# A graph network over 100,000 edges: of two steps' running maxima one row is stored, chosen by a masked copy

## The chip, the core and the metric

The kernel runs on one core of a Trainium2 chip. The core has TensorE (PE, matrix products into PSUM), VectorE (DVE, elementwise), ScalarE (ACT), GpSimd (POOL, which here issues the gathers) and SyncE (SP, which issues DMAs). Each engine works through its own list of instructions in order, and waits on semaphores for the others. The metric is the device time of one execution in microseconds (us). Before the change its median over 9 runs is 3999.06 us (3992.29 to 4028.08).

## The reference, cut to what matters

There are N = 6250 nodes with D = 256 features, E = 100,000 edges (src, dst, 64 edge features), and the edges come sorted by dst. Three times, the rows of the source nodes are gathered and their maximum is taken over all edges with the same dst:

```python
# 1: L0_gnn
e = relu((x[dst] - x[src]) @ theta_w.T + theta_b + x[src] @ phi_w.T + phi_b)
x = layernorm(x + where(isfinite(out := segment_max(e, dst, N)), out, 0))
# 2 and 3: L1_gnn, two rounds
hv = x @ W_in + b_in
for W, b in ((W_u0, b_u0), (W_u1, b_u1)):
    msg = segment_max(relu(concat([hv[src], edge_attr_64]) @ W + b), dst, N)
    hv = where(has_in, msg + hv, hv)
x = layernorm(x + relu(hv @ W_ro + b_ro))
```

The nodes have unequal numbers of edges; in the inputs given here one node has no edge and three have exactly one.

## The kernel before, in words

**Tables.** The product with a node's features is made once a node and not once an edge: each of the three sweeps r = 0, 1, 2 has a table in DRAM, `table[r]`, with one row of 256 numbers a node, and an edge fetches the row of its source. Table 0 is made in the prologue (L460 to 593), tables 1 and 2 by the nodes of the sweep before (L926 and the like). In the sweeps 1 and 2 the edge's own 64 features are multiplied and added for each edge.

**Edges.** They are taken in reverse order, padded to 782 x 128 and cut into 14 blocks (13 of 56 steps, one of 54). Within a block each of the 128 lanes (partitions) holds consecutive edges, one a step. So a node's edges lie behind one another in a lane, and may go on in the next lane, or in the next block.

**A step** (the loop at the end of `sweep`, L1010 to 1066). POOL gathers 128 rows of the table, one a lane, into a slot of a `run` tile of eight steps (`sources`, L784 to 792; four such tiles; issued AHEAD = 16 steps early). In sweeps 1 and 2 PE multiplies the features of two steps into a PSUM bank (`pair`, L816 to 831, three banks, issued two pairs early), and DVE adds the gathered rows to the bank (L1030, 512 elements a lane for two steps). Then one DVE instruction a step makes the running maximum along the lane (L1043, 256 elements): `lim` is large where the step's edge has the same dst as the one before and very negative where a new node begins, so the running maximum starts anew there. The result overwrites the gathered row. In sweep 0 a part of the steps takes raw rows of x and multiplies them itself (`raw_turn`, `raw_pair`); the others take table rows as they are.

**The store** (L1047 to 1051). After each eight steps SP stores the whole `run` tile, 1024 KB, to a DRAM array `S`, one row for every edge. The row at a node's last edge is the node's maximum within its lane.

**Block ends.** `over_lanes` (L833 to 860) transposes the lanes' last rows with PE, makes the running maximum over lanes with DVE and transposes it back into `cs` (the last KEPT = 6 blocks are held), so that a node that began in an earlier lane gets that lane's part too.

**Nodes** (L862 to 976). Tiles of 128 nodes, 49 a sweep. `rows` (L870) gathers with POOL the 128 rows of `S` at the nodes' last edges (`end_i`); it waits for all stores of `S` that are pending, and stands in POOL's list among the gathers of the steps. `picks` (L882) and `carried` (L889) fetch the carried part with one-hot matrices and PE, and the node's arithmetic follows in pieces, spread over some ten steps: the maximum (L931), adding (L935), two transposes (L760), a copy by ACT (L762), products (L768), biases (L926, L947), the layernorm (L746 to L755), and the rows of the next table or of the output.

**The order** is written by hand: a table of tasks by step number (`at`), the node schedule at L992 to 997. In sweep 0 DVE and PE also count the edges of each node with one-hot matrices (L707 to 722, the group L710, L716 and L721), 3 steps apart, up to step 320; from the counts `ends_a` and `ends_b` (L727 to 742) work out `end_i`, and only then, from step 324, can sweep 0's nodes begin; they follow at gaps of 6, later 3, steps.

**The check** (L538 to 567): DVE works out from the indices whether the edges are sorted and whether the nodes' tiles lie in the blocks for which the program was laid out. A value is loaded into a register (L588), and if it is not zero, another, general branch of the program (`any_order`) does the work. With the inputs given here the branch `in_order` is taken.

Of the kernel before, what the change touches and what calls it, by code (L numbers as in the profile page):

```python
# [8 lines left out]
F32 = mybir.dt.float32  # L9
BF16 = mybir.dt.bfloat16  # L10
I32 = mybir.dt.int32
# [6 lines left out]
P = 128  # L18
# [31 lines left out]
KEPT = 6  # L50
# [23 lines left out]
def gather_raw(nc, x, x_sb, s_r, i):  # L74

    nc.gpsimd.indirect_dma_start(out=x_sb[:, i, :], out_offset=None, in_=x,
                                 in_offset=bass.IndirectOffsetOnAxis(ap=s_r[:, i:i + 1], axis=0))

# [381 lines left out]
def gnn_kernel(  # L460
    ctx: ExitStack, tc: tile.TileContext, x, xT, src, dst, he, th_wT, th_b, ph_wT, ph_b,
    w_in, b_in, w_u0, b_u0, w_u1, b_u1, w_ro, b_ro, pos, heT, xTn, xn, w_inT, head, near, out,
# [51 lines left out]
    with tc.manual_schedule(), tc.tile_pool(name="pro", bufs=2) as pro, \  # L514
# [23 lines left out]
        def check():  # L538
            down = pro.tile([P, FS], F32, name="down", bufs=1)
            nc.vector.tensor_tensor(down, p_s, d_s, OP.is_lt)  # L540
            downs = pro.tile([P, 1], F32, name="downs", bufs=1)
            nc.vector.tensor_reduce(downs, down, AX.X, OP.max)
# [5 lines left out]
            nc.vector.tensor_max(downs[0:1, :], downs[0:1, :], bad)  # L548
            breaks_p = pps.tile([P, 512], F32, name="breaks_p", bufs=1)
            nc.tensor.matmul(breaks_p[:, :1], every, downs, start=True, stop=True)  # L550
            nc.vector.tensor_copy(breaks, breaks_p[:, :1])
            keep = pro.tile([P, FS], F32, name="down", bufs=1)
            nc.vector.tensor_tensor(keep, p_s, d_s, OP.is_equal)
            alike = BLOCKS.count(BLOCKS[0])
# [33 lines left out]
    bad = nc.values_load(breaks[0:1, 0:1], min_val=0, max_val=P)  # L588
# [8 lines left out]
def in_order(ctx: ExitStack, tc: tile.TileContext, g):  # L597
# [7 lines left out]

    nc = tc.nc
# [4 lines left out]
    part = g["part"]  # L611
# [4 lines left out]
    S = [dram_disjoint_views(nc.dram_tensor(f"S{r}", [FE, D], F32, kind="Internal").ap(), 2) for r in range(3)]  # L616
# [27 lines left out]
    winT = weight(g["w_inT"], "winT")  # L644
    wu0 = weight(g["w_u0"][:D, :], "wu0")
# [40 lines left out]
    def fuse_b():  # L686
        for b, w in ((b2, wu0), (bu1, wu1), (bro, wro)):
            ps = psum.tile([P, 512], F32, tag="pr", name="fuse_p")
            for k in range(2):
                nc.tensor.matmul(ps[:, :D], binT[:, k:k + 1].to_broadcast([P, P]), w[:, k, :], start=(k == 0),  # L690
                                 stop=(k == 1))
            nc.vector.tensor_add(b, b, ps[:, :D])
        nc.vector.tensor_add(tb, tb, pb)

# [48 lines left out]

    def stats(a, name):
# [12 lines left out]
    def turned(a):  # L757
        tp = psum.tile([P, 512], F32, tag="tp", name="tp")
# [12 lines left out]
    def sweep(r):  # L771
# [10 lines left out]
        runs = ahead.pop(r, {})  # L782

        def sources(s, r=r, runs=runs):  # L784
            if s % K == 0:
                runs[s // K] = work.tile([P, K, D], F32, name="run", bufs=4)
            if r == 0 and raw(s) is not None:
# [3 lines left out]
                out=runs[s // K][:, s % K, :], out_offset=None, in_=table[r][:SPARE + 1, :] if early else table[r],  # L791
                in_offset=bass.IndirectOffsetOnAxis(ap=(s_e if early else s_s)[:, s:s + 1], axis=0))

        def raw_turn(i):

            tp = psum.tile([P, 512], F32, tag="tp", name="tp")
# [36 lines left out]
        def over_lanes(b, last):  # L833

            lp = psum.tile([P, 512], F32, tag="tp", name="lp")
# [16 lines left out]
            def back():  # L852
                cp = psum.tile([P, 512], F32, tag="tp", name="cp")
# [8 lines left out]
        def node(t, g, b):  # L862
# [5 lines left out]
            def rows():  # L868
                o["m"] = work.tile([P, D], F32, name="m", bufs=7)
                i = nc.gpsimd.indirect_dma_start(  # L870
                    out=o["m"], out_offset=None, in_=S_r[:P * (FIRST[SPAN[t][1]] + BLOCKS[SPAN[t][1]]), :],
# [107 lines left out]
        if r == 0:  # L979
# [11 lines left out]
            at(begin - 1, ends_b)  # L991
        gap = (6, 4, 6)[r]  # L992
# [15 lines left out]
        for s in range(-AHEAD if r == 0 else 0, FS):  # L1008
# [15 lines left out]
            if s % 2 == 0:  # L1024
                two = runs[c][:, j:j + 2, :].rearrange("p s f -> p (s f)")
                if r > 0:
                    if s + 4 < FS:
                        pair(s // 2 + 2)
                    sums = hp.pop(s // 2)
                    nc.vector.tensor_add(sums, sums, two)  # L1030
                elif raw(s) is not None:
                    sums = hp.pop(s // 2)
# [7 lines left out]
            cur = runs[c][:, j, :]  # L1040
            row = sums[:, s % 2 * D:(s % 2 + 1) * D]
# [5 lines left out]
            if j == K - 1 or s in (FS - 3, FS - 1):  # L1047
                k = 2 if s == FS - 1 else j + 1
                to = S_w[P * FIRST[blk]:P * (FIRST[blk] + BLOCKS[blk]), :].rearrange("(p s) f -> p s f", p=P)
                at_ = s + 1 - k - FIRST[blk]  # L1050
                pending.append(nc.sync.dma_start(to[:, at_:at_ + k, :], runs[c][:, j + 1 - k:j + 1, :]))
# [67 lines left out]
```

## Time and profile before

| what | value |
| --- | --- |
| median of 9 runs | 3999.06 us |
| lowest, highest | 3992.29, 4028.08 us |
| the profiled execution's own time | 4036.09 us |
| its span in the trace | 4034.3 us |
| instructions in the span | 21650 |
| mean granted clock of PE | 0.684 |
| bytes moved | 739.39 MB, 183 GB/s over the span |
| of them, POOL's gathers (queue q0) | 326.92 MB, 27.1% of 16 DMA engines |
| of them, SP's queue, the stores among it (q1) | 337.85 MB, 22.4% |
| of them, ACT's queue, the edge features among it (q10) | 73.16 MB, 5.4% |
| HBM read, written | 404.56 MB, 333.17 MB |

The profile shows one execution, whose own time is 37 us above the median. Its rows give, for a group of like instructions, the line of the kernel, the engine, the operation, what is written and read, the number, the busy time in all and the mean duration in ns, and then the idle time of the engine just before them with what ended most of it. "remote" and "issue" stand for idle time that no instruction or transfer in the trace explains. The table by stage gives for a stretch of the span the busy time and number of instructions of each engine, then the granted clock, the share of the 16 DMA engines that was busy, and the rate. In a timeline the columns are the start, the duration, the engine, the line, the operation, and in brackets the idle time before it with what ended it. PE's ends are modelled and some records can be missing.

The three sweeps lie at about 0 to 1366, 1366 to 2720 and 2720 to 4034 us.

### The profile page before, as it was taken

To read this page: it belongs to the slowest core of one execution; us is meant where nothing else is said; L and a number is where in the kernel's file an instruction comes from. 1 tells how busy PE (TensorE), PEld (TensorE's weight loads), DVE (VectorE), ACT (ScalarE), POOL (GpSimd) and SP (SyncE) were. 2 spreads that over 40 slices of the span, in tenths; PEclk is the share of its full clock that TensorE was granted. 3 is DMA by queue.
4 is the path that set the end of the run, shared out by engine and by line. 5 is a ranking of instruction groups with operands and counts; after the bars stand their busy time and mean duration, and the time that the engine had idled before them with its cause. 6 is when DMAs were issued, how large, how long until landed. Compare 5 with 4: busy or idle time off the path is not lost. (4 is left out here: it accounts for less than half of the span.)

```text
span 4034.3 us, 21650 instructions
## 1 busy us (share of the span) xinstructions
PE 1857.2 (46%) x4631; PEld 821.8 (20%) x4631; DVE 2117.1 (52%) x4750; ACT 237.9 (6%) x618; POOL 2388.2 (59%) x2500
## 2 busy tenths in 40 slices
PE   5452223555520255454545445544545444444455
PEld 4341111222210122221212111122222121211111
DVE  1565554555543365554545456544655665555555
ACT  1000000111100000000000000000000000000000
POOL 5555556666666655655665566655555556666663
PEclk8665555655555577776767677767777878777767
DMA  6456545555555555555655555655555555555554
GB/s 239 161 180 203 187 146 177 176 168 184 169 187 167 177 198 184 188 176 173 201 170 189 166 188 203 211 177 182 180 179 179 184 188 187 189 183 188 189 197 159
DMA packets 241821, 739.39 MB, mean 183 GB/s; under 512 B 52485, under 2 KB 95858, under 8 KB 204434
## 3 DMA queue, kind: packets, MB, share of 16 engines
q0 software_dynamic: 119664, 326.92, 27.1%
q1 hardware_dynamic: 69568, 337.85, 22.4%
q10 hardware_dynamic: 52450, 73.16, 5.4%
q8 instruction: 39, 0.64, 0.1%
q14 instruction: 100, 0.82, 0.1%
HBM read 404.56 MB, written 333.17 MB: 183 GB/s over the span
## 5 line engine op out<-in xcount | busy, mean ns | idle before, releaser
L790 POOL DMA_INDIRECT run<-table,s_s x2258 | 2160.5, 957 | 1276.1 <-issue 656.6
L825 PE MATMUL hp<-whe,hT 128*128 128x512 f32 x1564 | 1007.5, 741 | 769.4 <-DVE run L1043 391.8
L1043 DVE SCALAR_TENSOR_TENSOR run<-run,lim,hp 128x256 f32<-128x256 f32 x1573 | 753.7, 479 | 58.7 <-remote 12.0
L1030 DVE TENSOR_TENSOR hp<-hp,run 128x512 f32<-128x512 f32 x782 | 542.2, 693 | 348.7 <-remote 190.2
L825 PEld LDWEIGHTS hp<-whe,hT 128*128 128x128 f32 x1564 | 298.7, 222 | 1306.9 <-DVE run L1043 725.1
L1043 DVE SCALAR_TENSOR_TENSOR run<-run,lim 128x256 f32<-128x256 f32 x731 | 351.5, 481 | 147.3 <-remote 48.5
L870 POOL DMA_INDIRECT m<-S,end_i x147 | 142.0, 966 | 311.7 <-DMA S<-run 205.3
L889 PE MATMUL v<-cs,pick 128*128 128x256 f32 (+1 forms) x438 | 169.1, 506 | 165.1 <-issue 72.3
L931 DVE TENSOR_TENSOR m<-m,v 128x256 f32<-128x256 f32 x98 | 40.5, 414 | 343.9 <-remote 223.6
L768 PE MATMUL prod<-wcat,aT 128*128 128x512 f32 x196 | 179.7, 1070 | 56.2 <-issue 39.5
L710 DVE TENSOR_TENSOR ol<-col,low 128x1024 bf16<-128x1024 bf16 x98 | 118.8, 1213 | 133.4 <-remote 123.2
L721 PE MATMUL hist<-oh,ol 128*128 128x8 bf16 (+7 forms) x782 | 34.8, 167 | 298.3 <-DVE oh L716 245.2
L889 PEld LDWEIGHTS v<-cs,pick 128*128 128x128 f32 x438 | 102.4, 255 | 274.4 <-issue 244.9
L768 PE MATMUL prod<-wro,aT 128*128 128x256 f32 x196 | 79.0, 543 | 171.6 <-ACT aT L762 88.5
L947 DVE TENSOR_TENSOR m<-prod,bro 128x256 f32<-128x256 f32 x49 | 20.8, 424 | 227.5 <-remote 93.9
L768 PE MATMUL prod<-wu,aT 128*128 128x256 f32 x196 | 72.0, 502 | 126.4 <-issue 79.1
L760 PE MATMUL tp<-ident,h_sb 128*128 128x128 f32 x196 | 48.3, 335 | 142.1 <-DVE h_sb L935 51.2
L926 DVE TENSOR_TENSOR new<-prod,b 128x256 f32<-128x256 f32 x49 | 20.8, 424 | 175.6 <-PE prod L768 71.6
L721 PEld LDWEIGHTS <-ol 128*128 128x128 bf16 x782 | 36.3, 104 | 323.0 <-DVE ol L710 229.6
L840 PE MATMUL lp<-ident,run 128*128 128x128 f32 x84 | 22.7, 363 | 169.5 <-DVE run L1043 98.0
L762 ACT COPY aT<-tp 128x256 f32<-128x256 f32 x147 | 54.7, 372 | 755.2 <-remote 403.1
L932 ACT ACTIVATE m<-m,has 128x256 f32<-128x256 f32 x98 | 49.7, 508 | 824.5 <-issue 386.7
(131 smaller groups left out, 1385.8 us busy)
## 6 DMA issues: line engine op xcount, KB each, us to landing
S<-run SPq DMA_DIRECT2D x291, 1024.0 KB
hT<-in_heT ACTq DMA_DIRECT2D x196, 256.0 KB
run<-table,s_s POOLq DMA_INDIRECT x2258
table<-new ACTq DMA_DIRECT2D x98, 128.0 KB
xg<-in_xTn SPq DMA_DIRECT2D x7, 896.0 KB
xT<-in_xTn SPq DMA_DIRECT2D x49, 128.0 KB
x_sb<-in_xn SPq DMA_DIRECT2D x7, 896.0 KB
out<-new ACTq DMA_DIRECT2D x48, 128.0 KB
```

What stands on the lines that cost most here:

```text
L710: nc.vector.tensor_tensor(ol[:, :k, :], col.unsqueeze(1).to_broadcast([P, k, P]), low[c // half][:, c % half * K:c % half * K + k].unsquee ...
L721: nc.tensor.matmul(hist[:, t0:t0 + w], ol[:, j, :], oh[:, j, :w], start=False, stop=(c == NG - 1 and j == k - 1))
L760: nc.tensor.transpose(tp[:, k * P:(k + 1) * P], a[:, k * P:(k + 1) * P], ident)
L762: nc.scalar.copy(aT.rearrange("p k e -> p (k e)"), tp[:, :2 * P])
L768: nc.tensor.matmul(ps[:, :n], aT[:, k, :], w[:, k, :], start=(k == 0), stop=(k == 1))
L790: nc.gpsimd.indirect_dma_start(out=runs[s // K][:, s % K, :], out_offset=None, in_=table[r][:SPARE + 1, :] if early else table[r], in_offs ...
L825: nc.tensor.matmul(hp[i], hT[c][:, q, :], whe[r - 1].rearrange("p s f -> p (s f)"), start=True, stop=not early)
L870: i = nc.gpsimd.indirect_dma_start(out=o["m"], out_offset=None, in_=S_r[:P * (FIRST[SPAN[t][1]] + BLOCKS[SPAN[t][1]]), :], in_offset=bass. ...
L889: nc.tensor.matmul(o["v"][:, :N1], p, cs[:, blk % KEPT, :N1], start=(blk == SPAN[t][0]), stop=(blk == SPAN[t][1]))
L932: nc.scalar.activation(o["m"], o["m"], AF.Relu, scale=has[:, t:t + 1])
L1030: nc.vector.tensor_add(sums, sums, two)
L1043: nc.vector.scalar_tensor_tensor(cur, prev, lim[:, s:s + 1], row, OP.min, OP.max)
```

## The change

**Of each two steps one row is stored.** A lane's two neighbouring steps 2q and 2q + 1 shall give one row of `S`. If the second edge belongs to the same node as the first, the row of the second step is kept: it contains the first. If a new node begins at the second edge, the row of the first step is kept: it is the end of its node. The second row is then lost for `S`; as long as the new node goes on in the next pair, nothing is lost by that, since its last row comes later. It is lost only if the node has one edge alone, at an odd position: a "lone" row.

For this the steps of a `run` tile are placed so that the even ones fill its first half and the odd ones its second (`slot`). Ahead of each store one DVE instruction, `copy_predicated`, copies the rows of the second half over those of the first half where the mask `goes_on` says so; the mask has one value a lane and pair, is spread over the 256 features by its access pattern, and lies in a PSUM bank of its own. The store takes the first half: 512 KB in place of 1024 KB, and `S` has one row for two edges and 128 rows more at its head.

**Lone rows are made on their own.** The lone nodes are found in sweep 0 from the counts (`ends_b`, `ends_c`), numbered, and their `end_i` points to the 128 rows at the head of `S`. `find` sends the position of each to the lane of its number: 49 one-hot picks by DVE and 49 matmuls with one column by PE. `found` gathers, from a new input `by_pos`, the features and the source of those edges; `found_b` makes the table index and transposes the features. In each sweep `lone_rows` gathers the 128 table rows and `lone_sums` adds the product of the features (sweeps 1 and 2) and stores the 128 rows. In sweep 0 all nodes start 21 steps later for this.

**The check** also counts the lone rows; if there are more than 128, the general branch is taken.

**Room.** KEPT goes from 6 to 7. The transposes' PSUM tag `tp` has one bank in place of two. Two weights, `winT` and `wu0`, needed until step 12 of sweep 0, lie in two of the four buffers of the tag `hT`.

The diff, with the check, the signatures and the unpacking of names left out:

```diff
-KEPT = 6
+KEPT = 7
+LONE = P
...
+def slot(s):
+    return s % 2 * (K // 2) + s % K // 2
...
-    S = [dram_disjoint_views(nc.dram_tensor(f"S{r}", [FE, D], F32, kind="Internal").ap(), 2) for r in range(3)]
+    S = [dram_disjoint_views(nc.dram_tensor(f"S{r}", [LONE + FE // 2, D], F32, kind="Internal").ap(), 2) for r in range(3)]
...
-    winT = weight(g["w_inT"], "winT")
-    wu0 = weight(g["w_u0"][:D, :], "wu0")
+    winT, wu0 = (work.tile([P, K // 2, P], F32, tag="hT", name=n, bufs=4).rearrange("p (k h) f -> p k (h f)", k=2)
+                 for n in ("winT", "wu0"))
+    nc.scalar.dma_start(winT, g["w_inT"].rearrange("(k p) f -> p k f", p=P))
+    nc.scalar.dma_start(wu0, g["w_u0"][:D, :].rearrange("(k p) f -> p k f", p=P))
...
+    goes_on = psum.tile([P, 512], F32, tag="on", name="goes_on", bufs=1)
+    nc.vector.tensor_scalar(goes_on[:, :FS // 2], lim.rearrange("p (q two) -> p q two", two=2)[:, :, 1], 0.0, None,
+                            OP.is_gt)
...
+        odd_i = one.tile([P, NT], I32, name="odd_i")
+        nc.vector.tensor_scalar(odd_i, end_i, 1, None, OP.bitwise_and)
+        nc.vector.tensor_scalar(end_i, end_i, 1, None, OP.arith_shift_right)
+        nc.vector.scalar_tensor_tensor(lone, cnt, 1.0, odd_i, OP.is_equal, OP.mult)
+        nc.vector.tensor_tensor_scan(incl, ones, lone, 0.0, OP.mult, OP.add)
+        ps = psum.tile([P, 512], F32, tag="pr", name="sums")
+        nc.tensor.matmul(ps[:, :1], above, incl[:, NT - 1:NT], start=True, stop=True)
+        sums.append(ps)
+    lone, number = (one.tile([P, NT], F32, name=n) for n in ("lone", "number"))
+    row = one.tile([P, DE + 2], F32, name="lone_row")
+    lone_s = one.tile([P, 1], I32, name="lone_s")
+    lone_T = one.tile([DE, P], F32, name="lone_T")
+    def ends_c():
+        base = one.tile([P, 1], F32, name="base")
+        nc.vector.tensor_copy(base, sums[1][:, :1])
+        nc.vector.scalar_tensor_tensor(number, incl, base, lone, OP.add, OP.mult)
+        nc.vector.tensor_scalar(number, number, -1.0, None, OP.add)
+        half = one.tile([P, NT], F32, name="half")
+        nc.vector.tensor_scalar(half, end_i, float(LONE), None, OP.add)
+        nc.vector.tensor_sub(incl, number, half)
+        nc.vector.tensor_mul(incl, incl, lone)
+        nc.vector.tensor_add(end_i, half, incl)
+    def find(t):
+        if t == 0:
+            sums.append(psum.tile([P, 512], F32, tag="pr", name="sums"))
+        p = work.tile([P, P], F32, name="pick", bufs=4)
+        nc.vector.tensor_scalar(p, col_f, number[:, t:t + 1], None, OP.is_equal)
+        nc.tensor.matmul(sums[2][:, :1], p, end[:, t:t + 1], start=t == 0, stop=t == NT - 1)
+    def found():
+        at_i = one.tile([P, 1], I32, name="at_i")
+        nc.vector.tensor_copy(at_i, sums[2][:, :1])
+        nc.gpsimd.indirect_dma_start(out=row, out_offset=None, in_=by_pos,
+                                     in_offset=bass.IndirectOffsetOnAxis(ap=at_i, axis=0))
+    def found_b():
+        of = row.bitcast(I32)[:, DE:DE + 1]
+        low_i = one.tile([P, 1], I32, name="low_i")
+        nc.vector.tensor_scalar(low_i, of, float(P), float(TROWS), OP.is_lt, OP.mult)
+        nc.vector.scalar_tensor_tensor(lone_s, of, float(-P), low_i, OP.add, OP.add)
+        ps = psum.tile([P, 512], F32, tag="tp", name="tp", bufs=1)
+        nc.tensor.transpose(ps[:DE, :P], row[:, :DE], ident)
+        nc.scalar.copy(lone_T, ps[:DE, :P])
...
-        tp = psum.tile([P, 512], F32, tag="tp", name="tp")
+        tp = psum.tile([P, 512], F32, tag="tp", name="tp", bufs=1)
...
+        def lone_rows():
+            alone["m"] = work.tile([P, D], F32, name="m", bufs=7)
+            nc.gpsimd.indirect_dma_start(out=alone["m"], out_offset=None, in_=table[r],
+                                         in_offset=bass.IndirectOffsetOnAxis(ap=lone_s, axis=0))
+        def lone_sums():
+            if r > 0:
+                ps = psum.tile([P, 512], F32, tag="pr", name="prod")
+                nc.tensor.matmul(ps[:, :D], lone_T, whe[r - 1][:DE, 0, :], start=True, stop=True)
+                nc.vector.tensor_add(alone["m"], alone["m"], ps[:, :D])
+            pending.append(nc.sync.dma_start(S_w[:LONE, :], alone["m"]))
...
-                out=runs[s // K][:, s % K, :], out_offset=None, in_=table[r][:SPARE + 1, :] if early else table[r],
+                out=runs[s // K][:, slot(s), :], out_offset=None, in_=table[r][:SPARE + 1, :] if early else table[r],
...
-                    out=o["m"], out_offset=None, in_=S_r[:P * (FIRST[SPAN[t][1]] + BLOCKS[SPAN[t][1]]), :],
+                    out=o["m"], out_offset=None, in_=S_r[:LONE + P * (FIRST[SPAN[t][1]] + BLOCKS[SPAN[t][1]]) // 2, :],
...
+            at(begin + 1, ends_c)
+            for t in range(NT):
+                at(begin + 2 + t // 7, find, t)
+            at(begin + 10, found)
+            at(begin + 14, found_b)
+            begin += 16
+        at(max(begin, EARLY + 4), lone_rows)
+        at(max(begin, EARLY + 4) + 4, lone_sums)
+        begin += 5 if r == 0 else 0
...
-                two = runs[c][:, j:j + 2, :].rearrange("p s f -> p (s f)")
+                two = runs[c].rearrange("p (two q) f -> p two q f", two=2)[:, :, j // 2, :]
...
-                to = S_w[P * FIRST[blk]:P * (FIRST[blk] + BLOCKS[blk]), :].rearrange("(p s) f -> p s f", p=P)
-                at_ = s + 1 - k - FIRST[blk]
-                pending.append(nc.sync.dma_start(to[:, at_:at_ + k, :], runs[c][:, j + 1 - k:j + 1, :]))
+                a, n = (j + 1 - k) // 2, k // 2
+                at_ = (s + 1 - k) // 2
+                nc.vector.copy_predicated(
+                    runs[c][:, a:a + n, :], goes_on[:, at_:at_ + n].bitcast(I32).unsqueeze(2).to_broadcast([P, n, D]),
+                    runs[c][:, K // 2 + a:K // 2 + a + n, :])
+                of, to = P * FIRST[blk] // 2, P * (FIRST[blk] + BLOCKS[blk]) // 2
+                to = S_w[LONE + of:LONE + to, :].rearrange("(p q) f -> p q f", p=P)
+                at_ -= FIRST[blk] // 2
+                pending.append(nc.sync.dma_start(to[:, at_:at_ + n, :], runs[c][:, a:a + n, :]))
```

## The prediction

> **What bounds the kernel now.** I read the page's totals and costliest groups first, then the waits, then single stretches of the timeline.
>
> ```profile
> PE 1857.2 (46%) x4631; PEld 821.8 (20%) x4631; DVE 2117.1 (52%) x4750; ACT 237.9 (6%) x618; POOL 2388.2 (59%) x2500
> ...
> L790 POOL DMA_INDIRECT run<-table,s_s x2258 | 2160.5, 957 | 1276.1 <-issue 656.6
> L1043 DVE SCALAR_TENSOR_TENSOR run<-run,lim,hp 128x256 f32<-128x256 f32 x1573 | 753.7, 479 | 58.7 <-remote 12.0
> L1030 DVE TENSOR_TENSOR hp<-hp,run 128x512 f32<-128x512 f32 x782 | 542.2, 693 | 348.7 <-remote 190.2
> L931 DVE TENSOR_TENSOR m<-m,v 128x256 f32<-128x256 f32 x98 | 40.5, 414 | 343.9 <-remote 223.6
> L710 DVE TENSOR_TENSOR ol<-col,low 128x1024 bf16<-128x1024 bf16 x98 | 118.8, 1213 | 133.4 <-remote 123.2
> ```
>
> No engine is full. POOL's gathers start 1.25 us apart (0.95 busy, 0.30 before the next), so 2493 of them need 3116 us of the 4034.3. DVE idles 1917 us, nearly all ahead of lines that read a PE product: L1030 348.7, L931 343.9, L947 227.5, L926 175.6, L710 133.4, L943 104.4, L900 84.4. For gathers it waits little (L1030 34.6 us). Averages hide that the sweeps alternate. One block (56 steps) of sweep 2, in the table by stage:
>
> ```profile
> core 0: us, PE busy (x) PEld busy (x) DVE busy (x) ACT busy (x) POOL busy (x), PEclk, DMA share, GB/s
> 3282.00:3333.00 51.00, 34.62 (x79) 13.57 (x79) 47.68 (x110) 5.40 (x15) 29.15 (x31) 0.93 0.66 221
> 3333.00:3377.00 44.00, 8.26 (x20) 4.50 (x21) 7.84 (x19) 1.30 (x4) 27.43 (x29) 0.60 0.45 144
> ```
>
> In the first stretch DVE is busy 47.68 of 51 us: it is the bound. In the second it does 7.84 us of work in 44. The timelines of DVE and POOL there:
>
> ```profile
> 3332.42 1.00 DVE L1043 SCALAR_TENSOR_TENSOR run<-run,lim,hp 128x256 f32<-128x256 f32 x2
> 3341.80 0.42 DVE L947 TENSOR_TENSOR m<-prod,bro 128x256 f32<-128x256 f32 x1 [8.38 <-remote]
> ...
> 3344.18 0.18 DVE L748 BATCH_NORM_AGGREGATE mv<-st 128x2 f32<-128x6 f32 x1
> 3357.90 0.42 DVE L931 TENSOR_TENSOR m<-m,v 128x256 f32<-128x256 f32 x1 [13.54 <-remote]
> ```
> ```profile
> 3315.81 0.94 POOL L870 DMA_INDIRECT m<-S,end_i  x1 [6.38 <-DMA S<-run]
> ...
> 3368.31 0.94 POOL L790 DMA_INDIRECT run<-table,s_s  x1 [0.30 <-issue]
> 3379.58 0.95 POOL L790 DMA_INDIRECT run<-table,s_s  x1 [10.32 <-DVE run L1043]
> ```
>
> DVE waits 8 to 14 us for PE products whose matmuls the profile shows as finished; the real ends are hidden, since PE's ends are modelled. POOL meanwhile issues without pause from 3315.81 until its run buffers are full at 3369, and DVE is free again at 3377.30, 8 us after POOL stops. Over the other blocks the timeline repeats this: PE turns slow some 17 to 21 us after POOL's last pause of 3 us or more, and recovers 6 to 10 us after the next. Why, no row says. For the sum it matters that the end of a slow stretch is timed by POOL, and that the fast stretch is DVE's.
>
> A rule to weigh here. The Trainium skill (TensorE: Matmul & The Clock Gate, Part 1) says that a quiet PE runs at half clock and is warm again after about 3.4 us of work. The 0.60 agrees with a half clock for part of the stretch, but half rate would make 8.26 us of matmuls 16 at most, not 44; by the page alone the slow stretch is no stall and would hide few copies, which is what I assume anyway.
>
> **The change, part by part.** The profiled execution took 4036.1 us (span 4034.3), 37.0 above the median of 3999.06; I sum against 4036.1 and take 37.0 off at the end.
>
> *The masked copy (added).* One DVE instruction of 4 x 256 = 1024 elements ahead of each store of eight steps, 294 to 297 in all. No row shows this operation. The nearest has as many elements: L710, 1213 ns. The f32 rows give the same: (693 - 414)/256 = 1.09 ns an element from L1030 and L931, so 414 + 768 x 1.09 = 1.25 us. Below: 0.69, if it passes two elements at a time (L1030's 512). Above: 2.43, if the selected write costs a second pass. I take 1.21. Behind it on DVE stand the next pair's L1030 and L1043, and SP's store waits for it. Where DVE is idle more than that in the same eight steps, it is hidden. I counted DVE's idle time between neighbouring stores (L1051) in the timeline: it is under 1.25 us in 60 groups of about 98 in sweep 1, 63 of 98 in sweep 2 and 17 of 96 in sweep 0, where PE's counting (L710 waits on it) and POOL leave 2 to 7 us a group. So 123 x 1.21 = **+149** and 17 x 1.21 = **+21**. The slow stretch doesn't absorb the copies ahead of it: DVE enters it some steps behind, POOL ends it at the same time, and those steps are then made up at DVE's pace.
>
> *The store (halved).* 291 stores of 1024 KB become 512 KB: about 154 MB less of 739. DMA is not full (0.66 in the fast stretch) and DVE doesn't wait for gathers, so bytes alone gain nothing. What gains is the landing, for which POOL waits at each block end:
>
> ```profile
> 3309.99 0.32 SPq L1051 DMA_DIRECT2D S<-run  x1
> ...
> 4019.19 0.32 SPq L1051 DMA_DIRECT2D S<-run  x1
> ```
>
> The first (1024 KB) frees POOL's gather at 3315.81, 5.82 us later; the last (256 KB) is followed by its gather at 4021.95, after 2.76. On the line between, 512 KB takes 3.78: 2.04 us less. One block end in each of 14 blocks of sweeps 1 and 2 is on the path, 28 x 2.04 = **-57**. At most all 46 waits of POOL for this store count (30 at L870, 16 at L790): -94; at least 0, if the later copy uses the time up. A rule speaks against halving: the Trainium skill (DMA: Bandwidth & Descriptors, Rules for kernel authors) wants at least 1 MiB a DMA, and its fit of 2.0 us plus bytes at 436 GB/s (Anatomy of one DMA) would save 1.2 us a store, an estimate of -34 in place of -57.
>
> *Lone rows and their search (added).* `find` is 49 picks of 290 ns (L882) and 49 small matmuls of two records each; L889's records are 0.38 us with 256 columns, its weight loads 0.19, so 0.4 to 0.76 us each: 14 us on DVE, 20 to 37 on PE, in seven steps of sweep 0, with four pick buffers between them. I take 15 on the path (0 where POOL's lead is the cover, 60 if a slow PE falls on it). Four gathers more are 4 x 1.25 = 5 us of POOL; the sums, the small stores on SP and the half-dozen index rows are some 3. Together **+23**.
>
> *Edits at no cost.* The check's extra rows (about 4 us by L540's 0.97) lie ahead of POOL's first run gather, which waits 23.4 us for the load of tb until 83.05; uncovered they cost 4. The first node of sweep 0 starts 21 steps later, but by the node schedule the backlog ends at step 636 either way. The slot order changes addresses only. One PSUM bank instead of two for the transposes lets the next wait for ACT's copy (L762, 372 ns); nodes are four steps or more apart, which covers it; uncovered, 147 x 0.37 = 54. Two weights in the hT buffers until step 12: 0 to 5.
>
> **Sum.** 149 + 21 - 57 + 23 = +136: 4036.1 + 136 = 4172, less 37 gives **4135 us**, 3.4% slower.
>
> **Rivals.**
>
> *PE's debt pays for the copies (faster).* If a slow stretch starts after so much PE work, and not after so much time, a slower DVE merely stretches the fast part, and copies fall into PE's 1418 us of waits. For it: the stretches return with the block. Against it: they come in sweep 0 too, with far smaller matmuls. The store's gain then stands alone: 3999 - 94 + 23 = 3928, or 3965 with -57. It decides when fewer than about 28 copies ((57 - 23)/1.21) stay on the path. Chance 0.17, and 0.03 for the next.
>
> *Slow stretches shrink with DMA traffic.* Fewer bytes (21%) would take 0.21 of them: 44 of each 95 us in 2668 us, about 1236, so -260 against +136: about 3875. Against: no store is in flight for most of them, and the DMA share is lower there (0.45).
>
> *A copy of 2.43 us.* 140 x 2.43 = 340 in place of 170: 4305. Only the missing row speaks for it. Chance 0.12.
>
> *About even.* Half of the 140 copies hidden and all 46 landings gained: 85 - 94 + 23 = +14, near 4013. Chance 0.13, of it 0.08 within 0.3% of before.
>
> *The fallback.* More than 128 lone rows would send the kernel into the other branch. The inputs have 3 nodes of one edge, none at an odd position: out.
>
> **How the numbers follow.** The forecast, 4060 to 4270, has 0.55 (copies of 0.69 us on 140 groups, 97 - 57 + 23, make 4062; 1.21 us on six of seven groups of sweeps 1 and 2, and on half of sweep 0's, with no store gain makes 3999 + 203 + 58 + 23 = 4283, cut at 4270). The range 3950 to 4270 leaves out the costly copy (0.12) and the lower part of the faster cases (0.08). About 0.3% is what this measurement can tell from no change: faster 0.20, same 0.08, slower 0.72 (0.55 + 0.12 + 0.05).
>
> **What would show it.** Copies of 1.2 us in DVE's groups; fast stretches of 51 us grown to about 57, slow ones still near 44; POOL's waits for S shorter by 2 us each; POOL's waits for DVE's run longer. I am wrong if the fast stretch keeps its length with the copies in it, if DVE's idle time falls by what the copies add, or if slow stretches get rarer.

## The result and the profile after

The changed kernel takes 4095.31 us (median of 20 runs, 4081.74 to 4108.57), the kernel before 4007.67 us over all 62 runs that stand beside it (3970.11 to 4049.50; the 3999.06 of the table above is the median of nine of them). The ratio is 1.0225, interval 1.0208 to 1.0241: about 90 us slower. The prediction said 4135 us, 3.4% slower.

The profiled execution took 4091.2 us (span 4089.4). From the page of the kernel after, the totals, the queue of the stores and the costliest groups that answer to those shown of before, with the copy as a new one (columns as before: number, busy time, mean ns, idle time before it):

```profile
PE 1901.9 (47%) x4736; PEld 864.2 (21%) x4736; DVE 2495.5 (61%) x5120; ACT 238.4 (6%) x619; POOL 2389.4 (58%) x2504
...
q1 hardware_dynamic: 70000, 184.49, 12.4%
...
L1142 DVE SCALAR_TENSOR_TENSOR run<-run,lim,hp 128x256 f32<-128x256 f32 x1573 | 753.4, 479 | 67.6 <-remote 17.5
L1129 DVE TENSOR_TENSOR hp<-hp,run 128x512 f32<-128x512 f32 x782 | 542.4, 694 | 139.6 <-remote 94.5
...
L1150 DVE COPY_PREDICATED run<-goes_on,run 128x1024 f32<-128x1024 int32 (+1 forms) x297 | 380.8, 1282 | 24.3 <-remote 8.8
...
L1021 DVE TENSOR_TENSOR m<-m,v 128x256 f32<-128x256 f32 x98 | 40.6, 415 | 347.4 <-remote 237.5
...
L739 DVE TENSOR_TENSOR ol<-col,low 128x1024 bf16<-128x1024 bf16 x98 | 118.6, 1210 | 67.0 <-remote 58.8
```

A copy takes 1.28 us; the 297 of them make 380.8 us, and DVE's busy time grew by 378.4. But the span grew by only 55.1: DVE's idle time fell from 1917 to 1594 us. The idle time ahead of L1030, now L1129, fell from 348.7 to 139.6, and ahead of L710, now L739, from 133.4 to 67.0; ahead of L931, now L1021, it stayed. SP's queue moved 184.49 MB in place of 337.85.

The table by stage for the three sweeps, first of before, then of after:

```profile
0.00:1372.00 1372.00, 532.65 (x1935) 299.39 (x1935) 656.39 (x1622) 112.91 (x286) 816.83 (x842) 0.58 0.54 180
1372.00:2695.00 1323.00, 670.26 (x1340) 260.54 (x1340) 696.64 (x1439) 55.13 (x141) 790.58 (x835) 0.72 0.56 187
2695.00:4034.00 1339.00, 654.25 (x1356) 261.90 (x1356) 764.09 (x1691) 69.82 (x191) 780.79 (x824) 0.75 0.55 183
```
```profile
0.00:1381.00 1381.00, 556.18 (x2036) 321.89 (x2036) 791.22 (x1792) 113.48 (x287) 820.85 (x847) 0.58 0.45 143
1381.00:2716.00 1335.00, 663.50 (x1342) 263.52 (x1342) 816.51 (x1539) 55.13 (x141) 786.93 (x832) 0.75 0.46 146
2716.00:4089.00 1373.00, 682.17 (x1358) 278.79 (x1358) 887.76 (x1791) 69.79 (x191) 781.65 (x825) 0.75 0.45 141
```

The second number is the length. Sweep 0 grew by 9 us, sweep 1 by 12, sweep 2 by 34, while DVE's busy time (the third pair) grew by 135, 120 and 124. The profiled execution of before lies 28 us above its median and that of after 4 below; these 32 us can't be put to a sweep.

A fast and a slow stretch of sweep 2 after the change, by stage (those of before are in the prediction):

```profile
3208.00:3276.00 68.00, 46.15 (x93) 19.25 (x93) 64.12 (x134) 6.03 (x16) 33.91 (x36) 0.80 0.49 152
3276.00:3312.00 36.00, 8.34 (x16) 4.07 (x16) 5.77 (x15) 1.17 (x3) 23.95 (x26) 0.59 0.36 108
```

The fast stretch is still DVE's (64.12 of 68 us) and has grown from 51 to 68 us, the slow one has shrunk from 44 to 36. But the stretches don't hold the same steps: the fast one has 55 after and 49 before, so 1.24 us a step in place of 1.04, and seven copies of 1.28 us are 9 of its 17 us more; the slow one has 4 steps after and 6 before. Whole blocks, from one block's first step to the next one's, have grown less: blocks 2 to 10 of sweep 2, counted from 0, by 2.8 to 5.4 us each. In the other blocks from 2 to 12 of sweep 2 the slow stretches after are 27 to 37 us long; before, most were 40 to 45. So the change did not only lengthen the fast stretch: the slow one gave something back.

### The profile page after: what moved, and what is told of

Same layout as the page of the kernel before. It is cut to its first block, busy times and chain, and to the rows that moved or that the text cites. A ratio compares the mean times of both kernels' runs of the same rounds, so it can differ in the third digit from the quotient of the medians.

```text
span 4089.4 us, 22776 instructions
## 1 busy us (share of the span) xinstructions
PE 1901.9 (47%) x4736; PEld 864.2 (21%) x4736; DVE 2495.5 (61%) x5120; ACT 238.4 (6%) x619; POOL 2389.4 (58%) x2504
## 3 DMA queue, kind: packets, MB, share of 16 engines
q1 hardware_dynamic: 70000, 184.49, 12.4%
## 5 line engine op out<-in xcount | busy, mean ns | idle before, releaser
L915 PE MATMUL hp<-whe,hT 128*128 128x512 f32 x1564 | 1018.9, 753 | 781.3 <-DVE run L1142 301.2
L1129 DVE TENSOR_TENSOR hp<-hp,run 128x512 f32<-128x512 f32 x782 | 542.4, 694 | 139.6 <-remote 94.5
L915 PEld LDWEIGHTS hp<-whe,hT 128*128 128x128 f32 x1564 | 312.0, 231 | 1310.7 <-issue 829.8
L1150 DVE COPY_PREDICATED run<-goes_on,run 128x1024 f32<-128x1024 int32 (+1 forms) x297 | 380.8, 1282 | 24.3 <-remote 8.8
L1021 DVE TENSOR_TENSOR m<-m,v 128x256 f32<-128x256 f32 x98 | 40.6, 415 | 347.4 <-remote 237.5
L739 DVE TENSOR_TENSOR ol<-col,low 128x1024 bf16<-128x1024 bf16 x98 | 118.6, 1210 | 67.0 <-remote 58.8
L845 PE MATMUL prod<-wro,aT 128*128 128x256 f32 x196 | 87.2, 590 | 140.0 <-issue 103.1
L1033 DVE TENSOR_TENSOR new<-prod,bu 128x256 f32<-128x256 f32 x49 | 20.7, 422 | 162.5 <-remote 101.6
L837 PE MATMUL tp<-ident,x_sb 128*128 128x128 f32 x98 | 31.5, 424 | 182.3 <-DVE no L994 76.4
```

Source lines behind the costliest of these rows:

```text
L739: nc.vector.tensor_tensor(ol[:, :k, :], col.unsqueeze(1).to_broadcast([P, k, P]), low[c // half][:, c % half * K:c % half * K + k].unsquee ...
L837: nc.tensor.transpose(tp[:, k * P:(k + 1) * P], a[:, k * P:(k + 1) * P], ident)
L845: nc.tensor.matmul(ps[:, :n], aT[:, k, :], w[:, k, :], start=(k == 0), stop=(k == 1))
L915: nc.tensor.matmul(hp[i], hT[c][:, q, :], whe[r - 1].rearrange("p s f -> p (s f)"), start=True, stop=not early)
L1150: nc.vector.copy_predicated(runs[c][:, a:a + n, :], goes_on[:, at_:at_ + n].bitcast(I32).unsqueeze(2).to_broadcast([P, n, D]), runs[c][:, ...
```

## The experiments

Twelve runs were made. None of them met the slow stretches of the result again: they ran on four chips, and on each the kernel before takes 3214 to 3215.5 us. That is itself the first finding. The result is taken here to come from another chip; whether it was that, or another condition of one of these four, no run tells.

### The same two kernels on another chip

> The kernel before, unchanged, for its profile on the chip that the next runs use too. On a chip like that of the first profiles: about 4008 us, PE's signals in multiples of 0.7 us for some 40 us a block. On a chip like that of the runs with and without copy: 3215 us, and no such stretch.

> The changed kernel, unchanged. On a chip like the first: 1.0225 times before, 4095 us. On a chip like that of the runs with and without copy, the two copies there cost 168 us, so one costs 84: 3208 + 84 = 3292 us, 1.024 times before. If the second copy is dearer than the first, because POOL's gathers still cover the first: 3240 to 3270 us.

Measured: before 3215.45 us in the profiled execution and 3214.06 us as the median of 7 runs, without one stretch of the slow kind in sweeps 1 and 2; after 3253.30 us, ratio 1.0119 (1.0102 to 1.0136), which is the lower of the two expectations, 3240 to 3270. The table by stage for the sweeps of before, then of after, on this chip:

```profile
0.00:1091.00 1091.00, 513.65 (x1935) 291.93 (x1935) 653.14 (x1621) 113.78 (x286) 818.58 (x839) 0.61 0.68 227
1091.00:2145.00 1054.00, 680.73 (x1340) 274.56 (x1340) 702.21 (x1440) 55.16 (x141) 788.26 (x833) 0.80 0.71 233
```
```profile
0.00:1129.00 1129.00, 547.24 (x2036) 317.26 (x2036) 788.02 (x1790) 113.71 (x287) 817.09 (x840) 0.60 0.56 174
1129.00:2184.00 1055.00, 704.69 (x1342) 271.95 (x1342) 829.74 (x1541) 55.17 (x141) 789.85 (x834) 0.77 0.60 185
```

Sweep 0 takes 38 us more; sweep 1 takes 1055 us in place of 1054, though DVE has 127.5 us more to do (sweep 2, not shown, is also within 1 us). The waits of DVE say where that work went, before and then after:

```profile
DVE hp L1030 <- DMA run<-table,s_s: 424.2, 244, 4.5
DVE run L1043 <- DMA run<-table,s_s: 217.3, 157, 4.5
```
```profile
DVE hp L1129 <- DMA run<-table,s_s: 220.2, 267, 2.4
...
DVE run L1142 <- DMA run<-table,s_s: 64.8, 76, 1.9
```

On this chip POOL's gathers bound the kernel: 2493 of them 1.25 us apart are 3116 us of 3214. In these lines DVE waits 641.5 us for gathers before and 285.0 after, 356.5 us less, where the copies add 381. What is nearly free on this chip is not free on the chip of the result, where DVE waited little for gathers.

### The copy left out, and made twice

```diff
-                nc.vector.copy_predicated(
-                    runs[c][:, a:a + n, :], goes_on[:, at_:at_ + n].bitcast(I32).unsqueeze(2).to_broadcast([P, n, D]),
-                    runs[c][:, K // 2 + a:K // 2 + a + n, :])
```

For the second kernel the same three lines stand twice.

> The changed kernel without the masked copy: of each two steps the first row is stored, whatever the mask says, so nodes that end at an odd position get a wrong row. Store, lone rows and search stay. All theories start from 4095 us for the changed kernel. A, the prediction's (a slow stretch of PE is untouched by the copies, and those ahead of it count in full, 140 in all): 4095 - 170 = 3925 us, fast stretches of sweep 2 shorter by 7 copies, slow ones unchanged at 30 to 37 us. B, formed from the two traces (a slow stretch begins at step 26 of its block and ends when POOL pauses, after a fixed 44 gathers, so the three copies between POOL's start and step 26 are paid back by a shorter slow stretch): four of seven copies a block in 28 blocks, 143, and 22 in sweep 0, so 3930 us, with fast stretches back near 52 and slow ones back near 44 us. C (PE's own debt pays for nearly all copies, and the loss is from the rest of the change): 4070 to 4095 us.

> The changed kernel with every masked copy made twice, the second with the same result. A: the fast stretches have no idle time left on DVE, so each of the 196 copies of sweeps 1 and 2 adds its 1.28 us and about 30 of sweep 0 do: 4095 + 289 = 4384 us. B: four of seven a block, 143, and some 30 in sweep 0: about 4270 us, with slow stretches of sweep 2 shorter again, near 28 us. C: under 4130 us.

Measured: without the copy 3207.80 us, ratio 0.9979 (0.9971 to 0.9988); with two 3376.16 us, ratio 1.0502 (1.0486 to 1.0518). Beside the changed kernel's 1.0119, measured on another of these chips, the first copy costs 1.4% or 45 us and the second 123 us of the 380 us that each adds to DVE. Most of the first one's price falls in sweep 0: sweep 1 begins at 1122.9 us before the change, at 1122.9 without the copy and at 1160.7 with it. The numbers of the expectations were made for the other chip; what can be read is that copies cost little while DVE has waits for gathers to fill and nearly three times as much once these are used up.

> The changed kernel without the masked copy once more (of each two steps the first row is stored, whatever the mask says), since the first such run fell on a chip where the kernel before takes 3215 us. On a chip like that of the first profiles (before near 4008 us): A, all copies ahead of a slow stretch count: 4095 - 170 = 3925 us; B, the slow stretch gives three of seven back: 4095 - 118 = 3977 us (the 118 is what is left of +88 when the store's gain of 28 x 1.8 us and 20 us for the lone rows are taken out); C, the copies are nearly free: 4070 us or more. On a chip like that of the first such run: 0.998 times before again.

Measured, on a third chip of this kind: ratio 0.9976 (0.9967 to 0.9985), as before. The question it was meant for, the copies' price on the chip with slow stretches, stayed open.

### The whole tile stored

```diff
-    S = [dram_disjoint_views(nc.dram_tensor(f"S{r}", [LONE + FE // 2, D], F32, kind="Internal").ap(), 2) for r in range(3)]
+    S = [dram_disjoint_views(nc.dram_tensor(f"S{r}", [LONE + FE, D], F32, kind="Internal").ap(), 2) for r in range(3)]
...
-                of, to = P * FIRST[blk] // 2, P * (FIRST[blk] + BLOCKS[blk]) // 2
-                to = S_w[LONE + of:LONE + to, :].rearrange("(p q) f -> p q f", p=P)
+                of, to = P * FIRST[blk], P * (FIRST[blk] + BLOCKS[blk])
+                to = S_w[LONE + of:LONE + to, :].rearrange("(p s) f -> p s f", p=P)
...
-                pending.append(nc.sync.dma_start(to[:, at_:at_ + n, :], runs[c][:, a:a + n, :]))
+                both = runs[c] if n == K // 2 else runs[c].rearrange("p (two q) f -> p two q f", two=2)[:, :, a:a + n, :]
+                to = to[:, at_:at_ + k, :]
+                pending.append(nc.sync.dma_start(to if n == K // 2 else to.rearrange("p (two q) f -> p two q f", two=2), both))
```

> The changed kernel, copy included, with stores of 1024 KB: both halves of the run tile go to a larger S. The nodes still read where they read before, so they get wrong rows of the same size and number. A and B: the store's landing is back at 5.8 us after its issue and POOL's wait at each block end in sweeps 1 and 2 is 2 us longer: 28 x 2.04, so 4095 + 57 = 4152 us. If bytes as such counted (154 MB more on queues that are half busy), more than 4180 us. If the later start of POOL's gathers is used up by the slow stretch behind it: 4095 to 4105 us.

Measured: 3265.23 us, ratio 1.0151 (1.0133 to 1.0169), beside 1.0119 (1.0102 to 1.0136) with the half store: 0.3%, 10 us, with intervals that overlap a little. The 57 us didn't come: on this chip POOL is behind and hardly waits for the store, 8.5 us in all. Nor did 154 MB more of traffic cost anything like the 85 us of the rival: bytes are not the bound here either, with a DMA share of 0.6 to 0.7. What the whole store costs where the slow stretches are is untested.

### The lone rows left out

```diff
-            for t in range(NT):
-                at(begin + 2 + t // 7, find, t)
-            at(begin + 10, found)
-            at(begin + 14, found_b)
-            begin += 16
-        at(max(begin, EARLY + 4), lone_rows)
-        at(max(begin, EARLY + 4) + 4, lone_sums)
-        begin += 5 if r == 0 else 0
+            begin += 3
+        at(40, lambda: pending.extend(nc.sync.dma_start(S_w[:LONE, i * P:(i + 1) * P], every) for i in range(2)))
```

> The changed kernel without the search for lone rows and without making them (with these inputs there are none, so the result is that of the reference); two small stores fill the 128 rows at the head of S, and sweep 0's nodes start 3 steps later than before the change in place of 21. A and B: 23 us less, 4072 us. Rival: the search lies beside POOL's gathers and the nodes' backlog in sweep 0 ends at the same step, so nothing: 4090 to 4100 us.

Measured: ratio 1.0069 (1.0054 to 1.0083) in place of 1.0119: 16 us less, and nearly all of it in sweep 0, where sweep 1 begins at 1145.0 us in place of 1160.7. It goes with a wait that the sum didn't name. From the waits of POOL in the changed kernel, on the chip of its run above, and then without the copy:

```profile
POOL lone_row L809 <- DVE at_i L808: 13.0, 1, 13.0
```
```profile
POOL lone_row L809 <- DVE at_i L808: 1.2, 1, 1.2
```

The gather of `found` stands in POOL's list 16 steps ahead of where DVE is, so POOL stops for 13.0 us until DVE has come to it (25.9 us on the chip of the result). Without the copies DVE is there almost in time, and the lone rows cost nothing: sweep 1 begins at 1122.9 us with them and without the copy, as before the change. So the 16 us are not a price of the lone rows alone. In sweep 0 the copies without lone rows cost 22 us (1145.0 - 1122.9), lone rows without copies none, and both together 38.

### Three run tiles

```diff
-                runs[s // K] = work.tile([P, K, D], F32, name="run", bufs=4)
+                runs[s // K] = work.tile([P, K, D], F32, name="run", bufs=3)
```

> The kernel before with three run tiles in place of four, so that POOL gets at most 24 steps ahead of DVE in place of 32. B (a slow stretch of PE ends when POOL pauses because its tiles are full): on a chip with slow stretches POOL's long burst of 44 gathers ends about 8 gathers, 10 us, sooner, and with it the slow stretch: 35 of them in sweeps 1 and 2, so some 3650 us; if a burst stays short enough for no slow stretch to begin at all, 3300 us. Rival (the slow stretch has its own length, whatever POOL does): 3990 to 4100 us. On a chip without slow stretches: POOL's gathers bound the kernel, and less lead costs 0 to 3%: 3215 to 3310 us.

> The kernel before with three run tiles once more. On a chip with slow stretches: B, POOL's long burst and with it the slow stretch end about 10 us sooner, some 3650 us, or 3300 us if no slow stretch begins; rival, 3990 to 4100 us. On a chip without them: 1.010 times before again.

Measured: 3245.10 us, ratio 1.0099 (1.0082 to 1.0115), and on another chip 1.0096 (1.0081 to 1.0112), as expected for a chip without slow stretches. Whether a shorter lead of POOL shortens the slow stretches could not be tried, since no such chip was met.

### A stop put in by hand

To have the fast and slow stretches of the first profiles on a chip without them, PE was held at the same place of each block by products that nobody reads:

```diff
+            if r > 0 and s - FIRST[max(i for i in range(NB) if FIRST[i] <= s)] == 23:
+                held = psum.tile([P, 512], F32, tag="pr", name="held")
+                for i in range(24):
+                    nc.tensor.matmul(held, ident, whe[r - 1].rearrange("p s f -> p (s f)"), start=True, stop=True)
```

> The kernel before with a stop of fixed length for PE put in by hand: at step 23 of each block of sweeps 1 and 2, 24 products of 512 columns whose sums nobody reads, 24 x 1.48 = 35.5 us, so that a block looks like one of the first profiles. DVE works some 55 to 60 us for a block and stands for most of the stop: blocks of 90 to 98 us in place of 76, 28 times 14 to 22 more: 3600 to 3830 us where the kernel before takes 3215. If POOL's lead hides the stops: under 3400 us.

> The changed kernel with the same stop. A (the copies ahead of a stop of fixed length count in full, as the prediction had it): 136 us above the kernel before with the stop, by the prediction's sum. B (on the first chip the stop was not of fixed length and gave copies back): here it can't, so the difference is larger than the 88 us of the first chip, 130 to 190 us. If the copies are hidden beside something else than the stop (POOL's gathers, as on this chip without the stop): 40 to 90 us.

> The changed kernel without the masked copy (of each two steps the first row is stored) with the same stop. A and B: 170 to 250 us under the changed kernel with the stop (140 to 196 copies of 1.28 us), and about 30 us under the kernel before with it (28 landings of 1.8 us less, 20 us for the lone rows more). If the copies are hidden: within 60 us of the changed kernel.

Measured: before with the stop 3308.27 us (1.0291, 1.0277 to 1.0306); after with it 3495.62 (1.0875, 1.0860 to 1.0890); without the copy 3276.93 (1.0197, 1.0183 to 1.0211). The stop was shorter than I had worked out, 20 to 22 us from its first product to its last in place of 35.5, and of 28 such stops, some 570 us, only 93 show in the time. That is the expectation's other case, a stop that POOL's lead mostly hides, so the stand-in before the change lies still near POOL's bound. The other two expectations hit: the change costs 187 us here, more than on the chip of the result; the copies alone cost 219, and what the change has besides them gains 31.

One block of sweep 2 with the stop, of before, of after, and without the copy:

```profile
2525.00:2609.00 84.00, 68.01 (x159) 29.47 (x157) 59.45 (x140) 6.93 (x20) 58.07 (x62) 0.92 0.66 217
```
```profile
2651.00:2742.00 91.00, 70.12 (x160) 30.14 (x160) 69.01 (x148) 7.34 (x21) 58.05 (x61) 0.89 0.52 157
```
```profile
2506.00:2588.00 82.00, 63.01 (x159) 27.30 (x157) 59.14 (x140) 6.89 (x19) 57.70 (x61) 0.98 0.57 176
```

DVE's busy time (the third pair) is 9.9 us longer with seven copies than without, and the block is 9 us longer: in this block, beside a stop of fixed length, the copies count in full. By sweeps, the changed kernel needs 72 us more in sweep 1, 112 in sweep 2 and 39 in sweep 0 than without the copy: 184 us in sweeps 1 and 2 of the 251 that 196 copies of 1.28 us make, 144 copies. And where POOL's gather of nodes waits for a store, it starts 6.15 us (median of 10) after the store's issue before the change, 4.08 us (of 9) without the copy but with half the store: 2.1 us less, close to the 2.04 of the line that the prediction drew.

## Why the prediction was right

**What bounds the kernel.** Right for the chip of the result, and it had to be: on four other chips the same kernel is bound by POOL, DVE waits for gathers, and half of what was argued here wouldn't hold. That DVE hardly waits for gathers and alternates between full and idle was read from this chip's trace and decides the sign of the copies' price.

**A copy of 1.21 us.** It took 1.28 us, 6% more; the row with as many elements was the right neighbour, and both ends, 0.69 and 2.43, are excluded.

**140 copies on the path.** The count was made of groups in which DVE had little idle time. With a stop of fixed length 144 copies count in sweeps 1 and 2 and some 30 in sweep 0 (39 us), where the prediction had 123 and 17. So in the stand-in more copies count than the prediction said. Whether the count was also too low on the chip of the result is not shown.

**"The slow stretch doesn't absorb the copies ahead of it."** This step failed. The prediction held that PE turns slow a fixed time after POOL's last pause, 17 to 21 us, and that slow stretches stay near 44 us. They are 36 us in the block shown and 27 to 37 in the others. The two traces agree on why, for sweep 2: in its blocks 2 to 10 the slow stretch begins at the same place of the work, step 26 or 27 of its block, in both kernels, be it 17 to 21 us after POOL's start (before, blocks 2 to 8), 31 and 37 (before, blocks 9 and 10, which the prediction's reading passed over) or 23 to 29 (after). And it ends when POOL pauses: the last of PE's late signals comes 6.8 us (median over sweeps 1 and 2) behind the end of POOL's last gather before and 6.7 after. In sweep 1 all blocks but the first behave so after the change, at step 25 or 26, but only six of 14 before it; the others begin elsewhere or have two stretches, and why is not shown. POOL's lines of block 5 of sweep 2 from the timeline, before and then after:

```profile
3218.55 0.94 POOL L870 DMA_INDIRECT m<-S,end_i  x1 [6.88 <-DMA S<-run]
...
3281.83 0.94 POOL L790 DMA_INDIRECT run<-table,s_s  x1 [8.58 <-DVE run L1043]
```
```profile
3252.79 0.94 POOL L960 DMA_INDIRECT m<-S,end_i  x1 [7.18 <-DMA S<-run]
...
3320.31 0.94 POOL L880 DMA_INDIRECT run<-table,s_s  x1 [12.74 <-DVE m L1021]
```

POOL starts at 3252.79 and issues 44 gathers until 3307.6, when its tiles are full; before the change it issued 44 too, from 3218.55 to 3273.3. That is 54.8 us in both. DVE comes to step 26 17.1 us after POOL's start before and 22.8 after: the three copies in between are 3.8 us of this, and the rest fits POOL's start, which follows the store some 2 us sooner. What is left of the 54.8 us is shorter by as much. DVE's lines in the slow stretch of the block before it:

```profile
3175.85 0.48 DVE L1142 SCALAR_TENSOR_TENSOR run<-run,lim,hp 128x256 f32<-128x256 f32 x1 [0.23 <-issue]
3194.74 0.42 DVE L1037 TENSOR_TENSOR m<-prod,bro 128x256 f32<-128x256 f32 x1 [18.41 <-remote]
...
3208.04 0.42 DVE L1021 TENSOR_TENSOR m<-m,v 128x256 f32<-128x256 f32 x1 [10.68 <-remote]
```

POOL's burst there ended at 3202.4, and DVE is free at 3208.04, 5.6 us later (before the change mostly 6 to 10 us later; after it, in blocks 6 to 11, only 0.2 to 3.1, and why is not shown). A part of what is given back is lost again: DVE leaves the stretch at step 27 to 30 of its block in place of 30 to 32, and these steps are made up behind it, as the prediction said. So it saw that POOL ends the stretch, and missed that in these blocks its beginning is fixed in the work and not in time. This account rests on the two traces alone. The runs with the stop fit it, a stop that can't give back and the same change 187 us dearer in place of 88, but they ran on another chip with a shorter stop, and don't prove it.

**The store's landing, 2.04 us each.** The size is right. POOL's gather of nodes that waits for a store starts 5.65 us (median of 20 in sweeps 1 and 2) after its issue before and 3.62 us (of 18) after, on the chip of the result: 2.0 us; 2.1 with the stop. That 28 of these make the time 57 us shorter is not shown. The Trainium skill (DMA: Bandwidth & Descriptors, Anatomy of one DMA) gave 1.2 us for it, an estimate from its fit, which is for DMAs that GpSimd issues, and this store is SP's; the measurement is nearer to the line drawn through two landings of this case. Its rule against DMAs under 1 MiB did not bite: with half the store the changed kernel takes 1.0119 times before, with the whole one 1.0151.

**Lone rows, +23.** Measured 16 beside the copies and nothing without them, on the other chips. The sum was near by luck and its reason wrong: it counted picks and products, and the time goes with POOL's wait for DVE at `found`, 25.9 us on the chip of the result, whose price there no run shows.

**The sum.** In the profiles, sweeps 1 and 2 grew by 46 us where the sum says 149 - 57 = 92, and sweep 0 by 9 where it says 21 + 23 = 44. The slow stretch that gives back doesn't account for that: in the 15 blocks whose slow stretch begins at steps 25 to 27 in both kernels, a block grew by 4.2 us in the mean (2.3 to 8.0), where the sum says 92/28 = 3.3. There the sum is near, though it has nothing given back in it and fewer copies than the stand-in counts. The growth is missing in sweep 0, and in the other 13 blocks, which together are 15 us shorter; before the change many of these have a stretch elsewhere or two. Why stays open, and 28 us of it may be that the profile of before was above its median. So the forecast, 40 us high, lies inside its range in part by luck.

**The signs that were named.** The copies take 1.28 us and the fast stretches grew, as said. One sign of being wrong came near: DVE's idle time fell by 323 us where the copies add 381; +136 us would have left a fall of some 245.

**The rivals.** "PE's debt pays" had its condition right for most of sweep 2, where the slow stretch starts after so much work, and its result wrong: the kernel got slower, since POOL sets the end and only the copies between POOL's start and step 26 are given back. "Slow stretches shrink with DMA traffic" has its 3875 us against it. But the stretches of sweep 2 did shrink by about a quarter, near the fifth that it names; the later coming of step 26 accounts for more than half of that, and the whole store, which would have tried it, did not meet a chip with slow stretches. As a part of the cause it is not excluded. The copy of 2.43 us and the fallback are out. "About even" is what happened on the other chips in sweeps 1 and 2, for a reason that it did not name, POOL's bound.

No version here beats both kernels: the only one faster than before, by 0.2%, leaves out the copy and with it a part of the result.

## What to carry to other kernels

Work added to an engine that idles half the time is free only if the idle time lies next to it: count it group by group, as was done here, and then ask of each stall what fixes its start and what fixes its end, since a stall that starts with the work and whose end is fixed by another engine can give back a part of what is added ahead of it. Compare whole blocks, or stretches with the same steps. A gather placed in the list of an engine that runs far ahead waits for whatever it reads, even if it costs 1.25 us itself. Two additions can cost together what neither costs alone, as the copies and the lone rows do in sweep 0. And a profile shows one chip: run the kernel before on another one if you can, since the engine that bounds it can be another there.

## What the runs showed of the hardware

**The same kernel takes a fifth less elsewhere.** It took 4007.67 us where the result was measured, 3214 to 3215.5 us on four chips later. The granted clock is 0.684 in the first profile and 0.738 on the second chip, too little a difference for it.

**What slow means.** In the slow stretches of the first chip the trace's counter of PE's signals rises at intervals that are whole multiples of 0.7 us. For the stretch of after shown above, from 3167.42:

```
signal at   3178.62 3183.52 3194.72 3201.02 3205.92 3208.02 3209.44
interval us   11.20    4.90   11.20    6.30    4.90    2.10    1.42
x 0.7            16       7      16       9       7       3       -
```

The first interval ends with a pair's product of 512 columns, which by the timeline began at 3168.62, so it took some 10 us; the last is one too, after the stretch, at 1.42 us. (This trace holds 1540 of 2212 such signals, that of the second chip 2208, so some intervals can span more than one.) Other slow stretches of both kernels show the same 0.7 us, each with its own offset, and the last such signal comes mostly 5 to 7 us after the end of POOL's last gather of the burst in sweeps 1 and 2. The Trainium skill (TensorE: Matmul & The Clock Gate, Seeing it yourself) tells of a gate stuck at a quarter for more than 50 us; a quarter would make at most 5.7 us of 1.42, an estimate, and some 10 were measured, so that doesn't cover it. On the other chips POOL issues without such pauses nearly all the time and PE shows nothing of the kind. So POOL's unbroken issuing goes with the slow stretches on one chip and is not enough for them on the others; what it is on that chip that slows PE stays open, and so does why it begins at step 26 in sweep 2.

**A masked copy of 128 x 1024 f32** with its mask spread from PSUM takes 1.28 us: 1.25 ns an element, close to what an f32 operation with two inputs takes (1.09 ns by the rows of the prediction), so the masked write costs no second pass.
